# Cross attentions: contraction of 192 as 128 rows plus two rests of 64 side by side, with keys first in the first turn

## The chip, the cores and the metric

The kernel runs on one core of a Trainium2 chip. The metric is the device time of one execution in microseconds (us); lower is better. The engines of a core are called PE (matrix engine; its weight loads are PEld), DVE (vector), ACT (scalar), POOL and SP (which issues most transfers).

## The reference

A decoder of two layers works on x of shape (8, 256, 256): in layer 0 a Mamba-like block, a cross attention and a mixture of experts, in layer 1 a rotary attention, a second cross attention and a split attention, each followed by a layer norm. All is float32. What matters here is the cross attention, whose context ctx_768 has shape (8, 77, 192):

```python
q = (x @ Wq).reshape(B, Nq, 16, 64)
k = (context @ Wk).reshape(B, 77, 16, 64)
v = (context @ Wv).reshape(B, 77, 16, 64)
attn = softmax(einsum('bqhd,bkhd->bhqk', q, k) / 8)
out = einsum('bhqk,bkhd->bqhd', attn, v).reshape(B, Nq, 1024)
return out @ Wo + bo
```

Keys and values contract over the 192 columns of the context, and there are 8 x 77 = 616 context rows.

## The kernel before

The function `cross` (line 300) is called twice, once per layer. It doesn't form q or the attention's output by head. It folds Wq into the keys and Wo into the values, so that x is multiplied directly with "weighted keys" M, and the probabilities directly with "weighted values" U:

- `keys(q, part)` (line 391): the keys of two batches (2 x 77 = 154 context rows) for four pairs of heads. A pair of heads fills 128 columns of Wk. The 192 rows of the contraction are two chunks of 96 rows (`kc`), so each pair of heads takes two matmuls that add up in PSUM (L399). The result is copied by ACT with the factor 1/8 into KT (L405).
- `weighted_keys(q, g)` (line 410): for each head, 64 rows of the keys against Wq. The two heads of a pair stand on partitions 0 to 63 and 64 to 127 and run side by side on PE (`tile_position`, L417). ACT copies M (L423).
- `values(c, g)` (line 333): the same as keys, for chunk c of 128 context rows (the fifth has 104) with Wv (L342); the copy VT is done by `evac`, which alternates between ACT (L74) and DVE (L76).
- `weighted_values(c, g)` (line 351): 64 rows of VT against Wo, two heads side by side (L361). `evac` copies U, and SP writes it to DRAM (`ud`, L374), since its rows are needed by batch and not by chunk; `load_U(b)` reads a batch's rows back (L383, L387).
- `scores(u)` (L436), `turn(u)` (transposes of the probabilities, L465) and `outputs(u)` (L481) work on unit u, that is half the heads of batch u // 2, 16 units in all.

PSUM has eight banks. The pool of `cross` has two buffers of one bank (`mm`: values, outputs, the transposes of x) and three buffers of two banks (`pair`, tag `sc`: scores, keys, weighted keys and values, turn).

The order is written out by hand. The first turn (`first`, line 509) prepares chunk 0 of the values, then the keys of batches 0 and 1, and puts pieces of the stage before (`tail`) at fixed places between:

```python
first = more[-2] + [lambda k=k: (keys, weighted_keys)[k // 2](0, k % 2) for k in range(4)]
places = (4, 5, 6, 7, 7, 8, 8)
```

Here `more[-2]` is values, values, weighted values, weighted values of chunk 0. After that comes the loop over units (line 525). In iteration u it issues scores(u + 1), outputs(u - 1), then one call of keys or weighted keys for a later pair of batches, then the pieces `more[u]` of the next chunks (values in u = -1, 1, 2, 4, 5, 8, 9; weighted values in 0, 3, 4, 6, 7, 10, 11), the transposes, and `after`, which belongs to the next stage. The first attention's tail is the end of mamba: the transposes and outputs of its last steps. In mamba's last step two pairs of PSUM banks are read late, by ACT (L234) and then by DVE (L242).

The weights arrive by `cross_weights` (line 1551) on SP's queue long before they are used, Wk and Wv as 96 partitions x 2 x 1024, the context as 96 partitions x 2 x 616.

Of the kernel before, what the change touches and what calls it, by code (L numbers as in the profile page):

```python
# [10 lines left out]
F32 = mybir.dt.float32  # L11
U32 = mybir.dt.uint32
I32 = mybir.dt.int32
AF = mybir.ActivationFunctionType
# [4 lines left out]
P = 128  # L19
NB, SEQ, D = 8, 256, 256  # L20
NT = NB * SEQ
NBLK = NT // P
NCTX, DCTX = 77, 192
EPS = 1e-5
BIG = 1e30
REG = 5
# [23 lines left out]
def decoder_kernel(ctx: ExitStack, tc: tile.TileContext, a: dict, out: bass.AP):  # L50
    nc = tc.nc
# [18 lines left out]
    def evac(dst, src):  # L70

        n_evac[0] += 1
        if n_evac[0] % 2:
            nc.scalar.copy(dst, src)  # L74
        else:
            nc.vector.tensor_copy(dst, src)  # L76
# [55 lines left out]
    def weight(pool, src, k, n, p=P, parts=1):  # L132

        t = pool.tile([P, 2048], F32, tag="w", name="w")
        v = t[:p, : k * n].rearrange("p (k n) -> p k n", k=k)
        rows = src.rearrange("(k p) n -> p k n", p=p)
        for i in range(parts):
            at = slice(i * n // parts, (i + 1) * n // parts)
            nc.sync.dma_start(out=v[:, :, at], in_=rows[:, :, at])
        return v  # L140
# [159 lines left out]
    def cross(xs, W, bias, ctxT, at_unit, after, tail):  # L300
# [5 lines left out]
        wv, wo, wk, wqT = W  # L306
# [4 lines left out]
        with ExitStack() as st:  # L311
# [7 lines left out]
            def mm():  # L319
                return cps.tile([P, 512], F32, tag="mm", name="mm")  # L320

            def pair():
                return cps.tile([P, 2, 512], F32, tag="sc", name="sc", bufs=3)
# [6 lines left out]
            def span(c):  # L330
                return c * P, min((c + 1) * P, NB * NCTX)

            def values(c, g):

                lo, hi = span(c)
                if g == 0:
                    VTs[c] = c1.tile([P, 8, P], F32, tag="VT", name="VT")
                ps = mm()
                for i in range(4):
                    hp = g * 4 + i  # L340
                    for kc in range(2):
                        nc.tensor.matmul(  # L342
                            ps[:, i * P : i * P + hi - lo], wv[:, kc, hp * P : (hp + 1) * P],
                            ctxT[:, kc, lo:hi], start=kc == 0, stop=kc == 1,
                        )
                evac(
                    VTs[c][:, g * 4 : g * 4 + 4, : hi - lo],
                    ps.rearrange("p (i n) -> p i n", i=4)[:, :, : hi - lo],
                )

            def weighted_values(c, g):

# [38 lines left out]
            def keys(q, part):  # L391

                if part == 0:
                    KTs[q] = c1.tile([P, 8, 2 * NCTX], F32, tag="KT", name="KT")
                ps = pair()
                for i in range(4):
                    hp = part * 4 + i
                    for kc in range(2):
                        nc.tensor.matmul(  # L399
                            ps[:, i // 2, i % 2 * 2 * NCTX : (i % 2 + 1) * 2 * NCTX],  # L400
                            wk[:, kc, hp * P : (hp + 1) * P],
                            ctxT[:, kc, q * 2 * NCTX : (q + 1) * 2 * NCTX],
                            start=kc == 0, stop=kc == 1,
                        )
                nc.scalar.activation(  # L405
                    KTs[q][:, part * 4 : part * 4 + 4].rearrange("p (a i) n -> p a (i n)", a=2),
                    ps[:, :, : 4 * NCTX], AF.Copy, scale=0.125,
                )

            def weighted_keys(q, g):  # L410
# [90 lines left out]
            more = {}  # L501
            for c in range(NCH):
# [3 lines left out]
                        lambda c=c, k=k: (values, weighted_values)[k // 2](c, k % 2)  # L506
                    )

            first = more[-2] + [
                lambda k=k: (keys, weighted_keys)[k // 2](0, k % 2) for k in range(4)  # L510
            ]
            places = (4, 5, 6, 7, 7, 8, 8)
            for i, piece in enumerate(first):
                piece()
                for t, at in zip(tail, places):
# [1034 lines left out]

    def cross_weights(pool, i, other=None):
        return (
            weight(pool, a[f"Wv{i}"], 2, 1024, 96), weight(pool, a[f"Wo{i}"], 8, D),
            weight(pool, a[f"Wk{i}"], 2, 1024, 96), weight(other or pool, a[f"Wq{i}T"], 8, D),
        )


    with ExitStack() as st:

        wx = st.enter_context(pool_of(tc, name="wx", bufs=3, side="right"))  # L1560
        cv = const.tile([P, 4, 6], F32, name="cv")
        w_bc = const.tile([P, 4, 32], F32, name="w_bc")
        ctxT = const.tile([96, 2, NB * NCTX], F32, name="ctxT")
        cst = const.tile([P, NCONST], F32, name="cst")
        cs = {n: cst[:, lo:hi] for n, (lo, hi) in _CONST.items()}
        rw = const.tile([P, 2, 8], F32, name="rw")
        rows = {
            n: const.tile([P, a[n].shape[0]], F32, name=f"row_{n}")
            for n in ("bo0", "ebias", "b_out", "bo1", "b_proj", "g0")
        }  # L1570
        route = Route(st, rw, rows["ebias"], cs)
        with pool_of(tc, name="wq", bufs=1) as wq:
            apart = ExitStack()
            wa = apart.enter_context(pool_of(tc, name="wa", bufs=3, side="right"))
            my = apart.enter_context(pool_of(tc, name="my", bufs=3, side="right"))
            load_x(0)
            w_in = weight(wa, a["W_inT"], 2, 1024, parts=4)
            for s in range(1, 4):
                load_x(s)
            nc.sync.dma_start(out=cv, in_=a["conv"].rearrange("(c p) k -> p c k", p=P))  # L1580
            nc.sync.dma_start(out=w_bc, in_=a["W_bcT"].rearrange("(c p) n -> p c n", p=P))
            W1 = (w_in, w_bc, weight(wa, a["W_dtT"], 4, 512), weight(wa, a["W_outT"], 4, D))
            nc.sync.dma_start(out=ctxT, in_=a["ctxT"].rearrange("(k p) n -> p k n", p=96))
            for n, t in rows.items():
                nc.sync.dma_start(out=t, in_=a[n].partition_broadcast(P))
            nc.sync.dma_start(out=cst, in_=a["consts"])
            nc.sync.dma_start(out=rw, in_=a["rwT"].rearrange("(k p) n -> p k n", p=P))
            W2 = cross_weights(wx, 0, wq)
            xs, tail = mamba(xs, W1, cv, my, apart.close)
            W3 = []  # L1590

            def shared_weights(u):
                for at, n, k, w in ((4, "sw1T", 2, 1024), (8, "sw2T", 2, 1024), (14, "sw3T", 8, D)):
                    if u == at:
                        W3.append(weight(wx, a[n], k, w))

            def routed(b, n_s, nT_s, ps):
                if b % 2:
                    route.add(b // 2, n_s, nT_s, ps)
                    if b < NB - 1:  # L1600
                        route.count(b // 2, ps)

            xs, tail = cross(xs, W2, rows["bo0"], ctxT, shared_weights, routed, tail)
        layer = ctx.enter_context(ExitStack())
        attention = ExitStack()

        def begin(xs):

            wc = layer.enter_context(pool_of(tc, name="wc", bufs=1))
            w6 = wc.tile([P, 2048], F32, name="w6")  # L1610
            signs = Signs(
                w6[:, 0:1536].rearrange("p (k n) -> p k n", k=2)[:, :, 0:256], rows["g0"], cs
            )
            wb = attention.enter_context(pool_of(tc, name="w4", bufs=1))
            w4 = wb.tile([P, 2048], F32, name="w4")
            W4, W6 = [], []
            for W, w, n, lo, hi in (
                (W4, w4, "wqkT", 0, 1024), (W4, w4, "wvT", 1024, 1536),
                (W4, w4, "woT", 1536, 2048), (W6, w6, "W_qkv", 0, 1536),
                (W6, w6, "W_proj", 1536, 2048),  # L1620
            ):
                v = w[:, lo:hi].rearrange("p (k n) -> p k n", k=2)
                nc.sync.dma_start(out=v, in_=a[n].rearrange("(k p) n -> p k n", p=P))
                W.append(v)
            rotary = Rotary(attention, xs, W4, cs)
            begun.extend([rotary, signs, W6])
            return rotary.first()

        begun = []
        xs, tail = experts(xs, W3, route, tail, begin)  # L1630
# [44 lines left out]
def _arrays(i):  # L1675

    def c(v):
        return np.ascontiguousarray(v)

    i = {k: np.asarray(v) for k, v in i.items()}  # L1680
    consts, rot = _constants()
    xp = i["L0_attn_W_xproj"]
    qkv = i["L1_attn_w_qkv"]
    return {
        "x": c(i["x"]),
        "ctxT": c(i["ctx_768"].reshape(NB * NCTX, DCTX).T),
        "consts": consts,
        "rot": rot,
        "W_inT": c(i["L0_attn_W_in"].T),
# [2 lines left out]
        "W_bcT": c(xp[:32].T),  # L1692
        "W_dtT": c(xp[32:].T),
        "W_outT": c(i["L0_attn_W_out"].T),
        **{f"W{n}{l}": c(i[f"L{l}_xattn_W{n}"]) for n in "kvo" for l in (0, 1)},
        **{f"Wq{l}T": c(i[f"L{l}_xattn_Wq"].T) for l in (0, 1)},
        **{f"bo{l}": c(i[f"L{l}_xattn_bo"]) for l in (0, 1)},
        "rwT": c(i["L0_ffn_router_w"].T),
# [42 lines left out]
```

## Time and profile before

| what | value |
|---|---|
| median of 5 runs | 1464.8 us (1462.6 to 1466.49) |
| profiled execution, time | 1464.22 us |
| profiled execution, span from first to last instruction | 1461.8 us |
| PE busy | 1383.5 us (95%), 7938 matmul instructions |
| DVE, ACT, POOL busy | 834.3, 654.7 and 522.1 us |
| mean granted clock of PE | 0.989 |
| first attention, first turn | 178 to 210 us |
| first attention, loop over units | 210 to 436 us |
| second attention, first turn | 957 to 978 us |
| second attention, loop over units | 978 to about 1200 us |

In a row of the profile, L342 is line 342 of the kernel; "out<-in" are the program's own names for tiles; x16 counts instructions; a time in brackets is how long the engine stood idle before the row, and who ended that. Each float32 matmul of the program appears as two matmul instructions and two weight loads.

### The profile page before, as it was taken

How to read it: one execution, taken by the hardware profiler on the slowest of the kernel's cores; microseconds unless marked ns; L12 is line 12 of the kernel's file. 1: busy time of each engine (PE TensorE's matmuls, PEld its weight loads, DVE VectorE, ACT ScalarE, POOL GpSimd, SP SyncE). 2: the span in 40 equal slices, each digit the busy share in tenths (PEclk: the TensorE clock that was granted, in tenths of full speed). 3: DMA queues.
4: the chain of work that ended last, by engine and by line, in shares of the span. 5: the costliest groups of instructions: out<-in, count | busy, mean ns of one | idle time of the engine just before them, and what ended most of it. 6: DMA issues, size and time to landing. Idle time of an engine off the chain costs nothing.

```text
span 1461.8 us, 21959 instructions
## 1 busy us (share of the span) xinstructions
PE 1383.5 (95%) x7938; PEld 966.8 (66%) x7938; DVE 834.3 (57%) x2285; ACT 654.7 (45%) x1608; POOL 522.1 (36%) x525
## 2 busy tenths in 40 slices
PE   8999889999999999999989999999999999899996
PEld 3443478888875666656566666678888787566564
DVE  3654445554662523323658888835555563787886
ACT  3555442333432112221248878833333322877884
POOL 0333122222210123316435665432333354546541
PEclk9999999999999999999999999999999999999999
DMA  9000023324350012332130000023222210100100
GB/s 246 24 0 1 0 93 94 107 73 161 111 222 15 22 44 87 86 121 82 29 101 2 1 1 2 1 83 117 80 75 86 76 41 6 19 16 16 30 16 16
DMA packets 71679, 87.81 MB, mean 60 GB/s; under 512 B 5588, under 2 KB 66164, under 8 KB 71060
## 3 DMA queue, kind: packets, MB, share of 16 engines
q1 hardware_dynamic: 68164, 77.10, 17.6%
q0 software_dynamic: 3408, 9.31, 2.3%
q8 instruction: 64, 1.05, 0.3%
q14 instruction: 43, 0.35, 0.1%
HBM read 56.87 MB, written 29.52 MB: 59 GB/s over the span
## 4 chain that ended last, share of the span: by engine, by line
PE 74%; DVE 15%; ACT 4%; POOL 4%; issue 3%; DMA 0%; POOLq 0%; DVEq 0%; ACTq 0%
PE mm L481 9%; PE sc L436 8%; PE mm L737 7%; DVE p L990 6%; PE mm L800 5%; PE op L1027 4%; PE ps_sc L1012 4%; PE pair L229 4%; PE ps_sc L981 4%; PE tr L754 3%; PE sc L399 2%; PE tr L814 2%; PE sc L417 2%; PE sc L465 2%; PE mm L342 2%
## 5 line engine op out<-in xcount | busy, mean ns | idle before, releaser
L997 ACT ACTIVATE p<-p,nmx 128x256 f32<-128x256 f32 x512 | 253.0, 496 | 64.4 <-DVE nmx L990 64.3
L456 POOL TENSOR_TENSOR p<-p,sm 128x616 f32<-128x616 f32 x60 | 72.6, 1215 | 249.1 <-DVE sm L453 218.7
L481 PE MATMUL mm<-Ub,pT 128*128 128x256 f32 (+1 forms) x640 | 144.6, 379 | 0.5 <-ACT pT L74 0.4
L436 PE MATMUL sc<-M,xT_s 128*128 128x308 f32 x512 | 139.6, 423 | 0.8 <-ACT pT L74 0.8
L1012 PE MATMUL ps_sc<-ident,p 128*128 128x128 f32 x1024 | 133.0, 277 | 6.7 <-DVE nmx L990 4.8
L1012 PEld LDWEIGHTS ps_sc<-ident,p 128*128 128x128 f32 x1024 | 114.6, 142 | 33.3 <-issue 13.1
L481 PEld LDWEIGHTS mm<-Ub,pT 128*128 128x128 f32 (+1 forms) x640 | 120.8, 190 | 20.0 <-ACT pT L74 0.9
L737 PE MATMUL mm<-xT_s,w 128*128 128x512 f32 x256 | 116.5, 608 | 3.8 <-DVE h L743 3.0
L436 PEld LDWEIGHTS sc<-M,xT_s 128*128 128x128 f32 x512 | 94.0, 188 | 33.4 <-ACT pT L74 1.5
L449 ACT ACTIVATE p<-p 128x616 f32<-128x616 f32 x64 | 45.8, 716 | 150.0 <-DVE p L445 128.5
L990 DVE CUSTOM_DVE_ANT_0 p<-ps_sc,zero 128x256 f32<-128x256 f32 x256 | 90.7, 420 | 29.1 <-PE ps_sc L981 27.6
L990 DVE CUSTOM_DVE_ANT_0 p<-ps_sc,term 128x256 f32<-128x256 f32 x256 | 90.6, 420 | 25.8 <-PE ps_sc L981 25.7
L997 ACT ACTIVATION_READ_ACCUMULATOR p<-p,nmx 128x1 f32 x512 | 96.0, 188 | 0.0
L774 POOL DMA_INDIRECT xb<-xd,token x39 | 37.2, 954 | 147.3 <-PE tr L781 81.1
L737 PEld LDWEIGHTS mm<-xT_s,w 128*128 128x128 f32 x256 | 48.8, 195 | 59.6 <-issue 54.5
L443 DVE TENSOR_REDUCE nmx<-sc 128x8 f32<-128x616 f32 x64 | 51.1, 798 | 54.5 <-PE sc L436 54.5
L1015 DVE COPY pT<-ps_sc 128x1024 f32<-128x1024 f32 x64 | 77.6, 1213 | 3.1 <-PE ps_sc L1012 3.1
L1015 ACT COPY pT<-ps_sc 128x1024 f32<-128x1024 f32 x64 | 63.7, 996 | 26.9 <-PE ps_sc L1012 26.7
L800 PE MATMUL mm<-wE,xbT 128*128 x156 | 73.5, 593 | 0.3 <-ACT xbT L786 0.3
L741 ACT ACTIVATE g<-mm 128x512 f32<-128x512 f32 x32 | 19.1, 597 | 104.5 <-PE mm L737 93.8
L452 DVE TENSOR_REDUCE sm<-p 128x8 f32<-128x616 f32 x64 | 50.6, 790 | 22.5 <-ACT p L449 21.9
L1270 POOL TENSOR_TENSOR ssq<-ssq,nhalf 128x32 f32<-128x32 f32 x8 | 43.4, 5430 | 54.7 <-DVE ssq L1267 54.7
(287 smaller groups left out, 2676.5 us busy)
## 6 DMA issues: line engine op xcount, KB each, us to landing
Ub<-ud SPq DMA_DIRECT2D x32, 512.0 KB
ud<-U SPq DMA_DIRECT2D x16, 616.0 KB
wE<-in_wE SPq DMA_DIRECT2D x4, 1536.0 KB
yd<-y SPq DMA_DIRECT2D x39, 128.0 KB
Ub<-ud SPq DMA_DIRECT2D x32, 104.0 KB
ud<-U SPq DMA_DIRECT2D x4, 608.0 KB
x_s<-in_x SPq DMA_DIRECT2D x8, 256.0 KB
w<-in_Wo SPq DMA_DIRECT2D x2, 1024.0 KB
```

What stands on the lines that cost most here:

```text
L229: nc.tensor.matmul(ps[:, i, :], w_dt[:, kc, c * P : (c + 1) * P], xc[s][kc // 2][:, kc % 2, :], start=kc == 0, stop=kc == 3,)
L436: nc.tensor.matmul(sc[:, a, : 4 * NCTX], xT_b[:, kc, j * P : (j + 1) * P], M[:, a * 4 : a * 4 + 4, kc, at : at + NCTX], start=kc == 0, sto ...
L456: engine.tensor_tensor(pv, pv, bcast(sm, 2, [P, 8, NCTX]), ALU.mult)
L481: nc.tensor.matmul(o[:, j * D : (j + 1) * D], pT[:n, c, j * P : (j + 1) * P],  Us[b][:n, g, c], start=g == 0 and j == 0 and c == 0, stop=g ...
L737: nc.tensor.matmul(ps, w[:, kc, cols], xT_s[:, kc, :], start=kc == 0, stop=kc == 1)
L800: nc.tensor.matmul(ps, xT[:, kc, :], column(j, kc * 512, 512), start=kc == 0, stop=kc == 1)
L981: self.last_score = nc.tensor.matmul(scs[s // 2][:, s % 2, :], self.queries(b, c, s, qb), self.keys(b, c, s), start=True, stop=True, tile_ ...
L990: self.last = nc.vector.tensor_tensor_reduce(out=p[:, h, :], in0=s4[:, h, :], in1=self.term(b, qb), scale=-1.0, scalar=3.0e38, op0=ALU.add ...
L997: nc.scalar.activation(p[:, h, :], p[:, h, :], AF.Exp, bias=nmx[:, qb, n : n + 1], scale=-1.0, accum_out=sums[:, qb, n : n + 1],)
L1012: nc.tensor.transpose(tr[:, at : at + P], p[:, h, kb * P : (kb + 1) * P], ident)
L1015: (nc.scalar.copy if j else nc.vector.tensor_copy)(self.pT[b, c, j][:, :, :, qb * P : (qb + 1) * P], tr.rearrange("p (h k t) -> p h k t", ...
L1027: nc.tensor.matmul(self.op[b][s * 32 : (s + 1) * 32, c, :], va[:, kb, 8 * c + 2 * s + m, :], self.pT[b, c, s // 2][:, s % 2 * 2 + m, kb, : ...
```

## The change

The contraction of 192 is cut differently: 128 rows in one full matmul, and a rest of 64. The rests of two pairs of heads stand on partitions 0 to 63 and 64 to 127 (the rest of the context is stored twice) and run side by side as two tiles of 64 rows. A new function, `from_context`, does this for keys and values; both now use the `pair` buffers, the two pairs of heads that run side by side going to different banks. The copy of the values of chunk 0 is always on ACT. The first turn now has the order keys, keys, values, values, weighted keys, weighted keys, weighted values, weighted values, and the tail's first two pieces come behind the second values. The weights are rearranged on the host into one chunk of 128 rows with 1024 + 512 columns.

```diff
+DHEADS = 1024
...
+            def from_context(w, g, lo, hi, copy, dst):
+                n, ps = hi - lo, pair()
+                for a in range(2):
+                    at = slice(a * n, (a + 1) * n)
+                    for i in range(2):
+                        hp = g * 4 + a * 2 + i
+                        nc.tensor.matmul(
+                            ps[:, i, at], w[:, 0, hp * P : (hp + 1) * P], ctxT[:, 0, lo:hi],
+                            start=True, stop=False,
+                        )
+                    for i in range(2):
+                        rest, k = DHEADS + (g * 2 + a) * P, slice(i * 64, (i + 1) * 64)
+                        nc.tensor.matmul(
+                            ps[:, i, at], w[k, 0, rest : rest + P], ctxT[k, 1, lo:hi],
+                            start=False, stop=True, tile_position=(i * 64, 0),
+                        )
+                copy(
+                    dst[:, g * 4 : g * 4 + 4, :n].rearrange("p (a i) n -> p i a n", a=2),
+                    ps[:, :, : 2 * n].rearrange("p i (a n) -> p i a n", a=2),
+                )
...
             def values(c, g):
-                ps = mm()
-                for i in range(4):
-                    hp = g * 4 + i
-                    for kc in range(2):
-                        nc.tensor.matmul(
-                            ps[:, i * P : i * P + hi - lo], wv[:, kc, hp * P : (hp + 1) * P],
-                            ctxT[:, kc, lo:hi], start=kc == 0, stop=kc == 1,
-                        )
-                evac(
...
+                from_context(wv, g, lo, hi, nc.scalar.copy if c == 0 else evac, VTs[c])
...
             def keys(q, part):
-                ps = pair()
...
+                from_context(
+                    wk, part, q * 2 * NCTX, (q + 1) * 2 * NCTX,
+                    lambda dst, src: nc.scalar.activation(dst, src, AF.Copy, scale=0.125), KTs[q],
                 )
...
-            first = more[-2] + [
-                lambda k=k: (keys, weighted_keys)[k // 2](0, k % 2) for k in range(4)
-            ]
-            places = (4, 5, 6, 7, 7, 8, 8)
+            first = [lambda k=k: (keys, weighted_keys)[k // 2](0, k % 2) for k in range(4)]
+            first[2:2], first[6:] = more[-2][:2], more[-2][2:]
+            places = (3, 3, 6, 7, 7, 8, 8)
...
-            weight(pool, a[f"Wv{i}"], 2, 1024, 96), weight(pool, a[f"Wo{i}"], 8, D),
-            weight(pool, a[f"Wk{i}"], 2, 1024, 96), weight(other or pool, a[f"Wq{i}T"], 8, D),
+            weight(pool, a[f"Wv{i}"], 1, 1536), weight(pool, a[f"Wo{i}"], 8, D),
+            weight(pool, a[f"Wk{i}"], 1, 1536), weight(other or pool, a[f"Wq{i}T"], 8, D),
...
-        ctxT = const.tile([96, 2, NB * NCTX], F32, name="ctxT")
+        ctxT = const.tile([P, 2, NB * NCTX], F32, name="ctxT")
...
+    def two_rests(w):
+        rest = w[P:].reshape(DCTX - P, 4, 2, P).transpose(2, 0, 1, 3).reshape(P, 4 * P)
+        return c(np.concatenate([w[:P], rest], 1))
...
-        "ctxT": c(i["ctx_768"].reshape(NB * NCTX, DCTX).T),
+        "ctxT": c(np.concatenate([ctxT, ctxT[P:]])),
```

More of the change, by code (lines that the diff above doesn't have):

```diff
@@ L337, in values @@
                     VTs[c] = c1.tile([P, 8, P], F32, tag="VT", name="VT")
-                ps = mm()
-                for i in range(4):
-                    hp = g * 4 + i
-                    for kc in range(2):
-                        nc.tensor.matmul(
-                            ps[:, i * P : i * P + hi - lo], wv[:, kc, hp * P : (hp + 1) * P],
-                            ctxT[:, kc, lo:hi], start=kc == 0, stop=kc == 1,
-                        )
-                evac(
-                    VTs[c][:, g * 4 : g * 4 + 4, : hi - lo],
-                    ps.rearrange("p (i n) -> p i n", i=4)[:, :, : hi - lo],
-                )
+                from_context(wv, g, lo, hi, nc.scalar.copy if c == 0 else evac, VTs[c])
             def weighted_values(c, g):
@@ L394, in keys @@
                     KTs[q] = c1.tile([P, 8, 2 * NCTX], F32, tag="KT", name="KT")
-                ps = pair()
[L396 to L407, printed above, removed]
+                from_context(
+                    wk, part, q * 2 * NCTX, (q + 1) * 2 * NCTX,
+                    lambda dst, src: nc.scalar.activation(dst, src, AF.Copy, scale=0.125), KTs[q],
                 )
@@ L1582, in decoder_kernel @@
             W1 = (w_in, w_bc, weight(wa, a["W_dtT"], 4, 512), weight(wa, a["W_outT"], 4, D))
-            nc.sync.dma_start(out=ctxT, in_=a["ctxT"].rearrange("(k p) n -> p k n", p=96))
+            nc.sync.dma_start(out=ctxT, in_=a["ctxT"].rearrange("(k p) n -> p k n", p=P))
             for n, t in rows.items():
@@ L1678, in c @@
         return np.ascontiguousarray(v)
+    def two_rests(w):
+        rest = w[P:].reshape(DCTX - P, 4, 2, P).transpose(2, 0, 1, 3).reshape(P, 4 * P)
+        return c(np.concatenate([w[:P], rest], 1))
     i = {k: np.asarray(v) for k, v in i.items()}
+    ctxT = i["ctx_768"].reshape(NB * NCTX, DCTX).T
     consts, rot = _constants()
@@ L1694, in _arrays @@
         "W_outT": c(i["L0_attn_W_out"].T),
-        **{f"W{n}{l}": c(i[f"L{l}_xattn_W{n}"]) for n in "kvo" for l in (0, 1)},
+        **{f"W{n}{l}": two_rests(i[f"L{l}_xattn_W{n}"]) for n in "kv" for l in (0, 1)},
+        **{f"Wo{l}": c(i[f"L{l}_xattn_Wo"]) for l in (0, 1)},
         **{f"Wq{l}T": c(i[f"L{l}_xattn_Wq"].T) for l in (0, 1)},
```

## The prediction

> **What bounds the kernel now.** I read the page first, then the sums over time windows for the two cross attentions, then TensorE's (PE's) timeline there.
>
> ```profile
> PE 1383.5 (95%) x7938; PEld 966.8 (66%) x7938; DVE 834.3 (57%) x2285; ACT 654.7 (45%) x1608; POOL 522.1 (36%) x525
> PE 74%; DVE 15%; ACT 4%; POOL 4%; issue 3%; DMA 0%; POOLq 0%; DVEq 0%; ACTq 0%
> ```
>
> PE is busy 95% and carries 74% of the chain. The window sums (columns: stretch, its length, busy us of PE, PEld, DVE, ACT, POOL, granted clock, DMA share, GB/s) ask whether that holds in the stages that change. The last two rows are the unit loops of both attentions, the first three lie in the first turn of the first.
>
> ```profile
> 182.83:186.25 3.42, 1.66 (x16) 1.46 (x16) 1.23 (x1) 1.69 (x3) 2.26 (x2) 1.00 0.00 0
> 186.25:189.66 3.41, 0.34 (x4) 0.00 (x0) 1.88 (x3) 1.01 (x1) 1.82 (x2) 1.00 0.00 0
> 189.66:193.07 3.41, 3.22 (x16) 2.54 (x16) 1.26 (x2) 1.01 (x1) 2.02 (x1) 0.50 0.26 75
> 211.00:436.00 225.00, 221.90 (x1376) 186.53 (x1375) 130.58 (x252) 77.73 (x112) 50.97 (x52) 1.00 0.40 130
> 978.00:1190.00 212.00, 208.19 (x1271) 174.19 (x1270) 124.05 (x208) 67.51 (x100) 76.97 (x54) 1.00 0.30 89
> ```
>
> In the loops PE idles 3.1 us of 225 and 3.8 of 212: there every ns added to PE's stream is a ns of the kernel. After a stretch with PE busy 0.34 us of 3.41 the clock is 0.50 for the next 3.41; after 1.66 of 3.42 (49%) it stays 1.00. The first turns wait (start, length, in brackets the idle time before):
>
> ```profile
> 178.10 3.74 PE L342 MATMUL mm<-ctxT,w 96*128 96x128 f32 x32
> 184.59 2.00 PE L361 MATMUL sc<-w,VT 64*128 64x256 f32 x16 [2.75 <-ACT VT L74]
> 189.85 3.57 PE L361 MATMUL sc<-w,VT 64*128 64x256 f32 x16 [3.26 <-DVE VT L76]
> ...
> 956.67 3.74 PE L342 MATMUL mm<-ctxT,w 96*128 96x128 f32 x32
> 963.20 5.41 PE L361 MATMUL sc<-w,VT 64*128 64x256 f32 x32 [2.79 <-DVE VT L76]
> 968.54 2.36 PE L399 MATMUL sc<-ctxT,w 96*128 96x154 f32 x16
> ```
>
> The weighted values (L361) wait for copies of the values that ACT and DVE do late; part of what follows runs at half clock (189.85: 3.57 us for x16, against 2.00). Now the prices, from rows of the loop:
>
> ```profile
> 226.54 3.72 PE L361 MATMUL sc<-w,VT 64*128 64x256 f32 x32
> ...
> 240.51 2.26 PE L399 MATMUL sc<-ctxT,w 96*128 96x154 f32 x16
> 242.60 1.95 PE L342 MATMUL mm<-ctxT,w 96*128 96x128 f32 x16
> ...
> 249.63 4.48 PE L481 MATMUL mm<-Ub,pT 128*128 128x256 f32 x20
> 254.04 2.37 PE L417 MATMUL sc<-KT,w 64*128 64x154 f32 x32
> 256.34 2.05 PE L342 MATMUL mm<-ctxT,w 96*128 96x128 f32 x16
> ```
>
> ```profile
> L399 PE MATMUL sc<-ctxT,w x256: 292/294/398, 193.3 to 1128.4; 96*128 96x154 f32 x128
> L417 PE MATMUL sc<-KT,w x512: 288/291/395, 198.6 to 1159.9; 64*128 64x154 f32 x171
> ```
>
> Each f32 matmul is two instructions. A slot is the distance of two starts: L399 (2.26 - 0.294)/15 = 0.131 us, L342 (1.95 - 0.275)/15 = 0.112. L417 works on 64 rows, two heads side by side: x32 are 16 pairs, (2.37 - 0.291)/15 = 0.139 a pair, so two for hardly more than the slot of one.
>
> The rest of that row is the price of **switching** between 128 and 64 rows. Out: the last pair of 254.04 starts at 254.04 + 2.37 - 0.291 = 256.12, the next row at 256.34, 0.22 later instead of 0.131 (0.09 lost); and that row takes 2.05 for what takes 1.95 after another 128-row matmul (0.10), because the first weight load is no longer hidden: 395 ns against 291 in L417's longest. In: row 249.63 last starts at 249.63 + 4.48 - 0.380 = 253.73, L417 0.31 later instead of 0.216 (0.09), and its row is 2.37 where 15 x 0.131 + 0.291 = 2.26 (0.11). A switch costs 0.19 to 0.20 us either way; I take 0.194.
>
> The Trainium skill (TensorEngine Tiling (Array Packing), Key Properties) says that changing the tiling mode drains TensorE, without a price; the rows above show the drain and its size. The same page's Theoretical Speedup table, up to 2x for contractions of at most 64, would alone promise the gross saving below with no cost, and about -23 us in all.
>
> **The change part by part.**
>
> *Fewer slots.* A call of values or keys had 8 matmuls = 16 slots; now 4 full ones (8 slots) and 4 of 64 rows in pairs (4 slots). Values: 20 calls x 4 x 0.112 = 9.0 us; keys: 16 x 4 x 0.131 = 8.4. Together -17.3.
>
> *More switches.* from_context goes full, rest, full, rest: in, out, in, out, four switches a call, unless weighted keys or values (already on 64 rows) follow, which saves one and removes one that was there. By units of the loop, new minus old: u=-1: 8, 0: 2, 1: 8, 2: 4, 3: 0, 4: 6, 5: 8, 6 and 7: 0, 8 and 9: 8 each: 52 per attention. First turn: 20 against 6 in the first attention, 18 against 4 in the second: 14 each. 2 x (52 + 14) = 132 x 0.194 = 25.6; 14 of them lead into transposes, whose load is shorter by 0.05: 25.0. So PE's stream grows by 25.0 - 17.3 = **7.7 us**.
>
> *First turn, second attention.* Keys first, value copies all on ACT. ACT is idle from 951.5 to 960.5 and the banks are free, so keys, values, weighted keys, weighted values run through: the idle 2.79 and the half clock (PEclk 0.5 for 3.41 us, worth 1.7) go, -4.4 with 0.1 for the tail's transposes, which need POOL's last row at 965.65 when PE arrives at 965.6. Scores start at about 974.6 instead of 978.01. U's round trip through DRAM on SP's queue starts 7.2 us later: weighted keys end at 971.0, the first half of the weighted values 1.73 and its copy 1.2 later, so 974.0 instead of 966.85. Its traffic ended at 990 before and should now at 997, and outputs of unit 0 need it at 999.3 (1002.22 before). Two us to spare, so nothing.
>
> *First turn, first attention.* The pool's first tag is now the three pairs, so these get the low six banks, handed out as first, third, second (so does every three-buffer tag in the program's memory map). The second keys call falls on the banks of mamba's last step, which DVE reads late:
>
> ```profile
> 184.09 1.23 DVE L242 SCALAR_TENSOR_TENSOR y<-pair,e 128x1024 f32<-128x1024 f32 x1 [2.35 <-ACT e L240]
> ```
>
> Keys 0 end at 178.10 + 12 x 0.131 + 4 x 0.194 = 180.45; keys 1 wait until 185.37: 4.9 us idle in one piece instead of 2.75 + 3.26, -1.1. Behind this wait stands PE's whole stream. PE is then busy 30% and 25% of the stretches to 182.83 and to 186.25, so I expect half clock until 189.66: 4.3 us at half, 2.15 lost against 1.6 now, +0.5. The 0.88 us before the next values (217.05, for a bank of mm that values no longer use) goes, -0.9. Together -1.4.
>
> *At nothing.* Values now share the three pairs with scores, keys and turns. The next scores take the buffer that values filled; the VT copy ended 0.2 to 1.0 us before scores began in eleven of the twelve places behind unit 0 and 0.2 after in one; the exit switch adds 0.15 of slack. What covers the copy is the turn's transposes; without them each place would cost what the copy is late. Wk, Wv and ctxT load in other shapes; they are issued by 24 and 744 us and used from 178 and 957 on. The copies' element counts stay.
>
> *Sum:* +7.7 - 4.4 - 1.4 = **+1.9 us**. The profiled execution took 1464.22 us (span 1461.8 and 2.4 around it), 0.6 under the median of the five runs, 1464.8. On the median: **1466.7 us**, +0.13%, less than the 0.2% (2.9 us) that a measurement can tell from no change.
>
> **The rivals.**
>
> *A. Side by side no longer hides* (slower). If scores wait for VT copies because these stand behind other work on ACT or DVE, these twelve places pay. A copy lasts 0.69 us and starts 0.04 to 0.56 behind the last matmul, against 1.24 of turn and switch; from 0.55 of delay on each further 0.4 costs 12 x 0.4 = 4.8 us: 1471.5. For: three pairs carry more than before; one place was late already. Against: eleven others.
>
> *B. U comes back too late in the second attention* (slower). Decides beyond 2.0 us of further delay; a stall of 2 to 4 us there gives 1469 to 1471. For: 23 us of round trip on one queue. Against: unit 0 needs only the first half of it.
>
> *C. The first attention doesn't wait* (faster). Were the early pairs on free banks, idle 6.0, half clock 1.6 and 0.9 all go: -8.5 instead of -1.4, 1459.6. If only the first values wait, -2.8 more than I sum: 1463.9. Against: the memory map.
>
> *D. Switches are cheaper in short runs* (faster). Without the exposed load, 132 x 0.10 = 13 us less: 1453. Against: mamba's bc_p matmul (two instructions on 16 rows between 128-row ones) pays both parts in full: 0.52 us from start to start into and out of it, against 0.43, and 0.10 more each time for the load.
>
> **How the numbers follow.** Forecast and its near variants (+-2.9 us) 0.47; A 0.26; B 0.08; C fully 0.07; D 0.05; longer half-clock or other new waits in the first turns, 1468 to 1470, 0.07. Slower: 0.26 + 0.08 + 0.06 = 0.40; faster 0.13; same 0.47. The range takes in A and B to 1472 and C in part, from 1461.5; the forecast's own is 1463.8 to 1469.6.
>
> **What would show it.** PE's instruction count unchanged at 7938; x8 of 128 rows and x8 of 64 in each call; about 25 us of drains and bare loads in PE's busy time, so units with keys and values longer by 0.5 us; scores in the second attention starting 3 to 4 us earlier against mamba's end, and the kernel giving it back by the loop's end; 4.9 us idle before the second keys at 185.4. I am wrong if switches cost under 0.15 us, if PE waits for VT copies in the loop, or if keys 1 start at 180.5.

## The result, and the profile after

The changed kernel takes 1468.84 us (median of 37 runs, 1460.5 to 1470.79) against 1464.77 us for the kernel before beside it (63 runs): a ratio of 1.0025 [1.0019, 1.0032]. So it is slower, by 4.1 us where 1.9 were forecast. The time lies within the forecast's own 1463.8 to 1469.6; but the difference can be told from none, and the prediction gave that less chance (slower, 0.40) than no difference that can be told (0.47). One execution of all those in this document, of e5, took 2012 us at a mean granted clock of 0.65, and no ratio counts it. The profiled execution took 1469.53 us, 5.3 more than that of before. First the engines and the chain in the page of after:

```profile
PE 1393.6 (95%) x7938; PEld 959.5 (65%) x7938; DVE 833.2 (57%) x2283; ACT 656.3 (45%) x1610; POOL 522.6 (36%) x525
PE 73%; DVE 16%; ACT 4%; POOL 3%; issue 3%; DMA 2%; SPq 0%; POOLq 0%; DVEq 0%; ACTq 0%
```

PE has the same 7938 instructions and is busy 10.1 us longer, in a span 5.4 us longer. Where, the distances between stage borders on PE's timeline tell, for both profiled executions:

| stretch | before | after | difference | forecast |
|---|---|---|---|---|
| up to the first matmul on the context (mamba) | 178.10 | 179.53 | +1.4 | 0 |
| first attention, first turn | 32.37 | 36.93 | **+4.6** | about +0.2 |
| first attention, loop (first scores to last outputs) | 224.63 | 226.23 | +1.6 | +2.2 |
| experts and rotary attention | 521.58 | 520.75 | -0.8 | 0 |
| second attention, first turn | 21.34 | 17.66 | **-3.7** | -3.7 |
| second attention, loop | 230.79 | 232.90 | +2.1 | +3.1 |
| rest | 253.0 | 253.2 | +0.2 | 0 |

The forecast column spreads the terms of the prediction over the stretches: 14 more switches in each first turn, 52 in each loop, less the slots saved there, with the waits and half clock that belong to each. The first and the fourth row hold no changed instruction. Stretches of half clock come there at other places in each execution, always of 3.41 us or a multiple of it (called windows here): the first row has one more of them after (from 112.70 us), the fourth four instead of three, and why that is still 0.8 us shorter is not settled. The four stretches that change give +4.6 us together, near the 4.1 of the medians. One row carries the miss: the first turn of the first attention. Its timeline in after (start, length, in brackets the idle time before and who ended it; L342 full part, L348 rest, L421 weighted keys, L89 transposes):

```profile
180.61 0.79 PE L342 MATMUL sc<-ctxT,w 128*128 128x154 f32 x4
181.33 0.53 PE L348 MATMUL sc<-ctxT,w 64*128 64x154 f32 x4
186.81 1.40 PE L342 MATMUL sc<-ctxT,w 128*128 128x154 f32 x4 [4.94 <-DVE y L243]
...
191.09 1.22 PE L342 MATMUL sc<-ctxT,w 128*128 128x128 f32 x4
...
198.61 1.97 PE L89 MATMUL mm<-ident,x_s 128*128 128x128 f32 x8
```

The wait is the forecast one: 4.94 us before the second keys, for DVE's late read of mamba's last buffer. But behind it every row has nearly twice its length (1.40 for the 0.79 of the same row ahead of the wait), and that lasts for all of the keys and values. The window sums of after say why (stretch, length, busy us of PE, PEld, DVE, ACT, POOL, granted clock, DMA share, GB/s):

```profile
181.00:184.38 3.38, 0.87 (x8) 0.47 (x6) 1.42 (x2) 3.35 (x3) 1.79 (x2) 1.00 0.00 0
184.38:187.79 3.41, 0.98 (x4) 0.98 (x4) 1.23 (x1) 1.11 (x2) 2.26 (x2) 0.50 0.00 0
187.79:191.21 3.42, 3.42 (x15) 2.18 (x14) 1.42 (x2) 0.68 (x2) 1.83 (x2) 0.50 0.02 5
191.21:194.62 3.41, 3.41 (x16) 2.73 (x16) 0.00 (x0) 0.68 (x1) 1.91 (x1) 0.50 0.01 2
194.62:198.03 3.41, 3.41 (x18) 2.51 (x16) 0.00 (x0) 0.58 (x1) 0.00 (x0) 0.50 0.00 0
198.03:201.45 3.42, 3.42 (x19) 2.86 (x21) 0.00 (x0) 1.75 (x3) 0.00 (x0) 0.50 0.00 0
201.45:204.86 3.41, 3.41 (x52) 3.36 (x52) 0.00 (x0) 3.06 (x6) 0.00 (x0) 1.00 0.00 0
```

The clock is 0.50 for five windows, 17.1 us, though PE counts as busy in all of the last four. Before, the full clock came back after one such window (189.66 to 193.07 in the prediction's rows). The second attention and the loop in after:

```profile
246.07 0.69 PE L342 MATMUL sc<-ctxT,w 128*128 128x154 f32 x4
...
250.46 1.31 PE L469 MATMUL sc<-ident,p 128*128 128x128 f32 x10
...
963.45 0.69 PE L342 MATMUL sc<-ctxT,w 128*128 128x154 f32 x4
...
965.71 0.79 PE L342 MATMUL sc<-ctxT,w 128*128 128x154 f32 x4
...
968.08 0.71 PE L342 MATMUL sc<-ctxT,w 128*128 128x128 f32 x4
...
972.33 0.69 PE L89 MATMUL mm<-ident,x_s 128*128 128x128 f32 x4
...
981.11 4.42 PE L440 MATMUL sc<-M,xT_s 128*128 128x308 f32 x16
```

A keys and a values call in one unit take 250.46 - 246.07 = 4.39 us; before, the same two took 244.39 - 240.51 = 3.88. That is +0.51, the 0.5 forecast for such a unit. In the second attention everything from the first keys (963.45) to the scores (981.11) runs through in 17.66 us without a wait.

### The profile page after: what moved, and what is told of

Read it like the earlier page. It is cut to its first block, busy times and chain, and to the rows that moved or that the text cites. A ratio compares the mean times of both kernels' runs of the same rounds, so it can differ in the third digit from the quotient of the medians.

```text
span 1467.2 us, 21969 instructions
## 1 busy us (share of the span) xinstructions
PE 1393.6 (95%) x7938; PEld 959.5 (65%) x7938; DVE 833.2 (57%) x2283; ACT 656.3 (45%) x1610; POOL 522.6 (36%) x525
## 3 DMA queue, kind: packets, MB, share of 16 engines
q1 hardware_dynamic: 67972, 77.26, 16.8%
## 4 chain that ended last, share of the span: by engine, by line
PE 73%; DVE 16%; ACT 4%; POOL 3%; issue 3%; DMA 2%; SPq 0%; POOLq 0%; DVEq 0%; ACTq 0%
PE mm L485 9%; PE sc L440 8%; PE mm L740 7%; DVE p L993 6%; PE mm L803 5%; PE op L1030 4%; PE ps_sc L1015 4%; PE pair L230 4%; PE ps_sc L984 4%; PE sc L342 3%; PE tr L757 3%; DVE acc L193 2%; PE tr L817 2%; PE sc L421 2%; PE sc L469 2%
## 5 line engine op out<-in xcount | busy, mean ns | idle before, releaser
L1000 ACT ACTIVATE p<-p,nmx 128x256 f32<-128x256 f32 x512 | 253.0, 496 | 64.9 <-DVE nmx L993 64.7
L993 DVE CUSTOM_DVE_ANT_0 p<-ps_sc,term 128x256 f32<-128x256 f32 x256 | 90.7, 420 | 26.5 <-PE ps_sc L984 26.4
```

Of the source, the lines that this page charges most:

```text
L993: self.last = nc.vector.tensor_tensor_reduce(out=p[:, h, :], in0=s4[:, h, :], in1=self.term(b, qb), scale=-1.0, scalar=3.0e38, op0=ALU.add ...
L1000: nc.scalar.activation(p[:, h, :], p[:, h, :], AF.Exp, bias=nmx[:, qb, n : n + 1], scale=-1.0, accum_out=sums[:, qb, n : n + 1],)
```

## The experiments

Two rounds of four kernels, each round with the kernel before beside it on its chip (1465.21 us in the first, 1464.6 in the second). A mode switch is counted wherever two matmuls that follow each other on PE use tiles of another size (128, 64 or 32 rows or columns): before 263, after 395, the forecast 132 more.

**e1: the order alone.** The kernel before, with its two chunks of 96 rows, and only the new order and the copies on ACT:

```diff
-            first = more[-2] + [
-                lambda k=k: (keys, weighted_keys)[k // 2](0, k % 2) for k in range(4)
-            ]
-            places = (4, 5, 6, 7, 7, 8, 8)
+            first = [lambda k=k: (keys, weighted_keys)[k // 2](0, k % 2) for k in range(4)]
+            first[2:2], first[6:] = more[-2][:2], more[-2][2:]
+            places = (3, 3, 6, 7, 7, 8, 8)
...
-                evac(
+                (nc.scalar.copy if c == 0 else evac)(
```

> The new order of the first turn alone (keys first, weighted values last, value copies of chunk 0 on ACT), with the old two chunks of 96 rows and values in the mm buffers. Theory T (the time is PE's stream: 0.194 us a switch of the row mode, against the slots saved): no switches added, loops as before within 0.5 us, second attention's first turn 16.8 instead of 21.3 us; in the first attention the second keys wait until DVE's late read as they do in the changed kernel (5.2 us idle). Theory H (the half clock after that wait lasted 17 us in the changed kernel because switches thin out PE's stream): a dense stream ends it within 3.4 to 6.8 us, first turn of the first attention 32 to 33 us, total 1460.2 (-4.6). If the length of the wait alone made it long: half clock about 17 us here too, first turn about 36, total 1464.5. Rival W (the cost lies in values on the shared pair buffers and copies over two banks): 1460.2 as well.

Measured: 1460.16 us (12 runs), 0.9967 [0.9955, 0.9979]. The order gains 5.0 us. In the profile 3.7 of that is the second attention's first turn (17.68 us, as in after, where 16.8 were expected: PE waits 0.9 us there for POOL's rows of the tail's transposes); the first attention's hardly changes (32.11 against 32.37 before). There PE waits 5.02 us before the second keys, as long as after does, and yet the clock is back after 6.8 us:

```profile
185.76 4.35 PE L399 MATMUL sc<-ctxT,w 96*128 96x154 f32 x16 [5.02 <-DVE y L242]
189.94 3.73 PE L342 MATMUL mm<-ctxT,w 96*128 96x128 f32 x32
```

The keys at 185.76 are at half clock (2.26 for the same row at 178.48), the values at 189.94 already at full (3.73, as in the prediction's row at 178.10).

**e2: the cut alone.** After, with the old order and places and `evac` for all value copies (the minus lines of e1's diff put back).

> The new cut alone (128 rows plus rests of 64) with the old order of the first turn and copies alternating as before. T: 132 - 2 = 130 switches more than before, +7.7 us of PE stream, and the second attention keeps its wait for DVE's copy (about 2.8 us): 1472.5. H: the second values now wait for DVE's late read, and a thinned stream follows: half clock over 10 us, 1475 to 1477. If the order costs and the cut gains: under 1464.8. W: 1470 to 1473, and PE waiting in the loops.

Measured: 1464.09 us (12 runs), 1.0005 [0.999, 1.002]: no difference that can be told, where a clear loss was expected. Its loops are longer by 1.7 and 2.0 us against before, as in after; its first turns by +1.6 and -1.6. That is +3.6 in the stretches that change, and the untouched experts and rotary stretch gives it back in this execution: it is 4.3 us shorter than in the profile of before, which had three windows of half clock there against one in e2. Over all runs the mean clock is 0.989 against 0.988, worth about 1.5 us of 1465; why the windows fall better in e2 than in before is not settled. Besides, the expectation put a longer half clock into the first turn, and it lasted 10.2 us, shorter than after's 17.1: dense weighted values (from 188.79 on) follow behind two values calls there. Two windows of e2:

```profile
186.00:189.40 3.40, 3.40 (x18) 2.64 (x19) 1.77 (x3) 0.00 (x0) 1.80 (x2) 0.50 0.02 5
189.40:192.80 3.40, 3.40 (x20) 2.70 (x18) 0.68 (x2) 1.01 (x1) 2.08 (x1) 0.50 0.01 2
```

Alone, the order gains 5.0 us and the cut costs nothing that can be told; together they lose 4.1. The two parts interact. Two theories for that: the long wait alone puts the clock down for long (then e1 should show it; it doesn't), or the stream behind the wait, broken by switches, keeps it down.

**e3: grouped.** After, but each call does its four full matmuls first and then the four rests, two switches instead of four:

```diff
-            def from_context(w, g, lo, hi, copy, dst):
+            def from_context(w, g, lo, hi, copy, dst, turned=False):
...
+                def whole(start):
+                    for a in range(2):
+                        at = slice(a * n, (a + 1) * n)
+                        for i in range(2):
...
-                            start=True, stop=False,
+                                start=start and a == 0, stop=not start and a == 1,
...
+                def rests(start):
...
-                            start=False, stop=True, tile_position=(i * 64, 0),
+                                start=start and a == 0, stop=not start and a == 1,
+                                tile_position=(i * 64, 0),
...
+                for part, start in zip((rests, whole) if turned else (whole, rests), (True, False)):
+                    part(start)
```

> As the changed kernel, but in each call all four full matmuls first and then all four rests: two switches a call, 72 fewer than the changed kernel, same matmuls, same buffers, same copies. T: 1468.8 - 72 x 0.194 = 1454.9. H adds that the half clock in the first attention's first turn gets shorter (under 10 us instead of 17), worth up to 4 us more: 1451. W (buffers and copies cost, not switches): 1468.8, no change.

Measured: 1454.1 us (6 runs), 0.9929 [0.9913, 0.9946], 14.7 us under after for 72 switches fewer. In the loop of the first attention 28 fewer switches take 226.23 to 220.79 us: 5.44 / 28 = 0.194 us each, the price that the prediction read from rows of before. The first scores and the last outputs of that loop, in after:

```profile
216.47 4.31 PE L440 MATMUL sc<-M,xT_s 128*128 128x308 f32 x16
438.11 4.59 PE L485 MATMUL mm<-Ub,pT 128*128 128x256 f32 x20 [0.40 <-ACT pT L75]
```

and in e3:

```profile
209.79 4.31 PE L450 MATMUL sc<-M,xT_s 128*128 128x308 f32 x16
425.99 4.59 PE L495 MATMUL mm<-Ub,pT 128*128 128x256 f32 x20 [0.40 <-ACT pT L75]
```

In the second loop only 3.2 of the expected 5.4 us show in the length; PE's idle time there is 5.3 us of 210 against after's 3.1 of 212, so 2.2 us turned into waits. And the half clock ends after 6.8 us, behind a wait of 5.34 (windows of e3):

```profile
183.31:186.72 3.41, 0.89 (x3) 0.89 (x4) 1.23 (x1) 1.20 (x2) 2.26 (x2) 0.50 0.00 0
186.72:190.14 3.42, 3.42 (x17) 2.80 (x17) 1.41 (x2) 1.19 (x2) 1.83 (x2) 0.50 0.02 5
190.14:193.55 3.41, 3.41 (x34) 2.92 (x34) 0.00 (x0) 0.95 (x3) 2.02 (x1) 1.00 0.01 2
```

W, which put the cost on buffers and copies, is out, since e3 has after's. That the total lies so near T's 1454.9 is partly luck. In the profile the first attention's first turn shrinks by 5.7 us (36.93 to 31.23), some 4 more than its eight switches are worth, as H said. But the second attention's, also with eight switches fewer, does not shrink at all (17.68 against 17.66), since PE now waits 1.3 us there for POOL's rows of the tail's transposes. What H adds and what these waits take back nearly cancel.

**e4: grouped and turned.** e3, and where two calls follow each other the second begins with its rests (`turned`), so that no switch lies between them (36 fewer again):

```diff
-                from_context(wv, g, lo, hi, nc.scalar.copy if c == 0 else evac, VTs[c])
+                from_context(
+                    wv, g, lo, hi, nc.scalar.copy if c == 0 else evac, VTs[c], c > 1 or g == 1
+                )
...
-                    lambda dst, src: nc.scalar.activation(dst, src, AF.Copy, scale=0.125), KTs[q],
+                    lambda dst, src: nc.scalar.activation(dst, src, AF.Copy, scale=0.125), KTs[q],
+                    q == 0 and part == 1,
```

> As e3_grouped, but every second call begins with its rests where the call before ended with them: 108 switches fewer than the changed kernel, only 24 more than before. T: 1468.8 - 108 x 0.194 = 1447.9, so some 17 us (1.2%) under the kernel before; H: half clock shorter, down to 1444. W: 1468.8.

Measured: 1453.31 us (6 runs), 0.992 [0.9902, 0.9937], 5.4 us above what was expected. The first loop gave its share, 220.79 to 218.62 us for 14 switches (0.155 each; several of them lead into transposes, whose load is shorter). The second attention did not: its first turn takes 19.13 us instead of 17.68, because PE arrives too early at the tail's transposes. The waits of PE between 950 and 985 us in e4 (what waited, for whom: us in total, times, longest):

```profile
PE mm L89 <- POOL x_s L117: 1.9, 2, 1.1
PE sc L387 <- DVE U L77: 0.8, 1, 0.8
```

A window of half clock follows the first of them, at 957.7; another, at 988.4, stands behind this 0.8 and a further wait of 1.83 us for the copy of U. A saving ahead of a fixed arrival became waits and slow windows. Over all six executions the mean clock is 0.984 to 0.988, against 0.989 or 0.990 in e3; 0.004 of 1453 us are 5.8, about what is missing. Two of the windows more lie in the experts in this execution, so not all of it is explained.

**e5: without most of the wait.** After, with mamba's first two transposes ahead of the keys in the first attention, so that the first buffers of both tags are taken in another order and the late-read bank falls to a later call:

```diff
-            places = (3, 3, 6, 7, 7, 8, 8)
+            places = (-1, -1, 6, 7, 7, 8, 8) if len(tail) > 2 else (3, 3)
+            for t, at in zip(tail, places):
+                if at == -1:
+                    t(mm())
```

> As the changed kernel, but in the first attention two of mamba's transposes are issued ahead of the keys, so that the mm buffers get the low banks and the pairs the others: both keys calls fall on free banks and only the first values wait for DVE's late read at 185.4. Switches the same. Theory TH (0.194 us a switch, and a half clock that the wait starts and the thinned stream prolongs): idle 1.7 us instead of 4.9, no 17 us of half clock, first turn of the first attention 27.6 instead of 36.9 us, total 1459.5. If the wait matters but not the half clock behind it: 1468.8 - 3.2 = 1465.6. W (buffers and copies): 1465.6 or more.

Measured: 1462.28 us (11 runs), 0.9988 [0.9976, 1.0], 6.6 us under after but 2.8 above what was expected. The wait is down to 1.70 us, the first turn from 36.93 to 29.06; 0.9 us of that is only the two transposes, which now stand ahead of the first keys. The expectation counted on no half clock; the values behind this short wait still ran at half for 6.8 us (timeline and windows of e5):

```profile
185.25 0.71 PE L342 MATMUL sc<-ctxT,w 128*128 128x128 f32 x4 [1.70 <-DVE y L243]
```

```profile
182.81:186.22 3.41, 1.71 (x15) 1.17 (x13) 1.22 (x1) 2.08 (x4) 2.26 (x2) 0.99 0.00 0
186.22:189.63 3.41, 3.37 (x18) 2.45 (x14) 1.41 (x2) 1.74 (x3) 1.82 (x2) 0.50 0.00 0
```

**e6: grouped, turned and ahead.** e4 and e5 together, and the second attention's transposes put two calls later, behind the weighted keys, to give POOL's rows time (`else (5,)` for `else (3, 3)`).

> e4_turned with the transposes ahead as in e5_ahead, and in the second attention the tail's transposes behind the second weighted keys, since PE waited 1.9 us there for POOL's rows and went to half clock. TH: first turn of the first attention 26.3 us instead of 30.6, of the second 16 instead of 19.1: 1445.4, the fastest. If only the idle time counts: 1453.3 - 3.6 - 1.9 = 1447.8. W: no difference to e4_turned beyond the idle time.

Measured: 1446.19 us (4 runs), 0.988 [0.9864, 0.9895]: faster than both kernels, 18.4 us under before and 0.8 from what was expected. The wait for POOL's rows is gone, the second attention's first turn is down to 15.59 us. The wait for mamba's bank in the first attention, in e6:

```profile
185.20 1.99 PE L344 MATMUL sc<-ctxT,w 128*128 128x128 f32 x8 [2.70 <-DVE y L243]
```

**e7: the order and the transposes ahead, old cut.** e1 with the diff of e5.

> e1_order (old cut into 96 + 96) with the transposes ahead. TH: first turn of the first attention 27 instead of 32.1 us: 1455.1; so e6_turned_ahead is 10 us faster than this one by fewer slots (-17.3) against 24 to 26 switches (+5) and what the clock adds. If the cut gave nothing: equal.

Measured: 1455.02 us (5 runs), 0.9934 [0.992, 0.9947], as expected. Here no half clock follows at all: the first turn takes 25.61 us, or 26.5 with the two transposes ahead of it, the shortest of all, with a wait of 1.27:

```profile
184.62 3.84 PE L342 MATMUL mm<-ctxT,w 96*128 96x128 f32 x32 [1.27 <-ACT xT_s L93]
```

So of e6's 18.4 us the order and the transposes' place bring 9.6, and the cut, once grouped and turned, 8.8 more. Up to 0.9 of these 8.8 is not the cut's: e7 keeps the second attention's transposes at their place in after and waits 0.9 us there for POOL's rows. By the terms, 17.3 of slots less 30 more switches than e7 (289 against 259), 30 x 0.194 = 5.8, would be 11.5. Part of the difference lies in the first attention's first turn, 26.96 us in e6 against 25.61: PE waits 2.70 us there and 3.4 us of half clock follow. Another part lies in the second loop, where PE waits 6.5 us in e6 and 5.0 in e7, most of it for copies of U.

**e8: grouped in the first attention's first turn alone.** After, with e3's grouping only in the four calls of this turn, one ahead of the wait and three behind it (`grouped = q == 0 and len(tail) > 2`, for values `c == 0 and len(tail) > 2`): 8 switches fewer than after, the wait kept.

> The changed kernel with the four calls of the first attention's first turn grouped (all full matmuls, then all rests): 8 switches fewer, at half clock some 2 us, the wait of 4.9 us before the second keys stays, all else the same. TH: half clock behind the wait 6.8 us instead of 17.1 as in e3_grouped, first turn 36.9 - 5.5 = 31.4 us, total 1463.2, mean clock up from 0.984 to 0.988. If the long wait alone sets the half clock: 17 us stay, and 1467.2 remains.

Measured: 1461.44 us (11 runs), 0.9975 [0.9966, 0.9984], 7.4 us under after and 1.8 under what TH gave. This separates the two theories. The wait is even longer than after's (5.34), and the half clock lasts 3.4 us instead of 17.1 (timeline and windows of e8):

```profile
185.34 2.42 PE L343 MATMUL sc<-ctxT,w 128*128 128x154 f32 x8 [5.34 <-DVE y L243]
187.69 1.23 PE L352 MATMUL sc<-ctxT,w 64*128 64x154 f32 x8
188.85 1.16 PE L343 MATMUL sc<-ctxT,w 128*128 128x128 f32 x8
...
192.32 1.09 PE L89 MATMUL mm<-ident,x_s 128*128 128x128 f32 x8
193.34 4.67 PE L439 MATMUL sc<-KT,w 64*128 64x154 f32 x64
```

```profile
181.80:185.21 3.41, 0.00 (x0) 0.00 (x0) 1.15 (x1) 2.22 (x2) 2.35 (x1) 1.00 0.00 0
185.21:188.62 3.41, 3.28 (x14) 2.97 (x16) 0.95 (x3) 0.68 (x1) 2.35 (x1) 0.50 0.02 5
188.62:192.03 3.41, 3.41 (x34) 2.89 (x34) 0.54 (x1) 1.27 (x2) 2.35 (x1) 1.00 0.01 2
```

The eight switches are worth at most 8 x 0.194 = 1.6 us at full clock; the first turn shrank by 6.1 (36.93 to 30.79). The other 4.6 are half clock that the order of eight matmuls within a call decides. The wait starts the half clock; the broken stream keeps it.

That it lasts 3.4 us here and 6.8 in e3, behind the same wait and the same calls, is where the windows fall: in e8 one begins at 185.21, just before the wait ends, in e3 the wait ends at 185.83, 2.5 us into one. In after it ends 2.4 us into one, as in e3, so of the four windows by which after and e8 differ one is luck and three are not. A single trace could mislead here, but the mean clock of the other executions agrees: 0.989 to 0.991 in all 11 of e8, 0.981 to 0.986 in 34 of the 39 of after whose clock is on record, and the two kernels differ in nothing else. The other five of after have 0.988 to 0.991 and take 1460.5 to 1466.8 us.

## Why the prediction was right in most steps and wrong in one

**Switches and slots: right.** PE's instructions are 7938 as said, the program has 132 more switches as counted, and 0.194 us a switch is what 28 of them gave in e3. The loops grew by 1.6 and 2.1 us where the terms make 2.2 and 3.1. What is missing is idle time that the longer stream of PE covered: PE idled 3.1 and 3.8 us in the windows of the loops before and idles 1.6 and 3.1 now (0.9 of the first is the gap that the prediction takes out). The windows of after:

```profile
217.00:442.00 225.00, 223.41 (x1373) 182.60 (x1372) 129.73 (x250) 77.62 (x112) 50.98 (x52) 1.00 0.41 135
982.00:1194.00 212.00, 208.91 (x1263) 168.98 (x1262) 123.00 (x206) 66.98 (x99) 76.01 (x53) 1.00 0.31 96
```

So the prediction erred a little high here: it let the switches add in full and forgot that a stream that gets longer waits less for the others.

**Second attention's first turn: right.** -3.7 forecast (the -4.4, and 0.7 for 14 switches less the slots), -3.68 measured.

**First attention's first turn: the wait right, its price wrong.** Rival C is out: the memory map was read rightly, and keys 1 stood 4.94 us for 4.9 forecast. The step that failed is "I expect half clock until 189.66: 4.3 us at half, 2.15 lost". It took from one row of before that one window of work releases the clock. Measured, the half clock lasted to 201.45. The loss, by rows of after at half and at full clock (those from 965.71 to 972.33 in its second attention): keys 4.28 against 2.37 us, each values call 3.76 against 2.12; the eight transposes take 1.90 against 1.02 in e8, and the weighted keys 0.4 more than in the second attention: 6.5 us in sum. That is 4.4 more than the 2.15, and the stretch missed by 4.4.

What keeps the clock down can be put in a number, an estimate from slots: at half clock a slot is about twice 0.131 or 0.112 us (e1's row of keys takes 4.35 us at half and 2.26 at full). The keys call at 186.81 has 12 slots, 12 x 0.262 = 3.14 us of its 4.28, 73%; a values call 12 x 0.224 = 2.69 of 3.76, 72%. The rest is drains and bare loads, which the rows still count as busy. Three windows of after filled with such calls did not release the clock; its fourth (198.03 to 201.45, mostly transposes and weighted keys, about 89%), e8's first (3.14 of 3.51, with the idle start about 86%), e1's (96% and more) and before's did. Windows that mix thin and dense rows lie close together by this estimate, 79% in e2 (not released) and 81% in e5 (released). So grouping decides, which e8 shows; that the share of streaming time is the measure, and where its threshold lies, is only argued from these estimates.

The Trainium skill (TensorE: Matmul & The Clock Gate, What's actually happening) says that the full clock comes after at least one busy window of about 3.4 us. The windows of 3.41 us are in these rows, and e1, e3 and e8 come near it, with one or two. After does not: of its four windows with PE busy all the time, three passed before one released the clock. So the busy time of the profile can't be what decides here.

**Rival A: refuted, by after's own trace.** The price of late VT copies was not paid. The waits of PE in the window of the second loop (what waited, for whom: us in total, times, longest), with none for VT; in the first loop there is none either (with the faster streams of e3 and e6 one of 0.4 and 0.7 us does appear in the second loop):

```profile
PE sc L469 <- DVE U L77: 2.3, 3, 1.0
PE sc L375 <- DVE U L77: 0.8, 1, 0.8
```

**Rival B: did not occur.** No wait for `Ub` stands at the second attention's first outputs. **Rival D: refuted.** The bare load is there in short runs too. The rests in after (instructions, durations in ns as least, median and most):

```profile
L348 PE MATMUL sc<-ctxT,w x288: 272/353/621, 180.2 to 1136.0; 64*128 64x154 f32 x64, 64*128 64x128 f32 x64, 64*128 64x104 f32 x16
```

The median mixes three sizes and both clocks, so take one size at full clock: of the 64 instructions on 154 columns in the second attention 32 last about 290 ns and 32 about 395, the usual and the longest duration of L417 before. The drawn-out matmul behind an unhidden load, which L417 had only in its longest ones, is every second instruction in runs of two pairs. And e3's 0.194 us a switch is the full price, not the 0.09 without the load.

**The sum.** +1.9 forecast, +4.6 in the four stretches: 4.4 more in the first turn, 1.6 less in the loops. That the time still lies in the forecast's range owes something to luck, since the two errors have opposite signs. The 0.07 given to "longer half-clock or other new waits in the first turns, 1468 to 1470" was the case that came; it deserved more, since all the switches of that turn stood behind the one wait, and the chance of the likeliest case, with its half clock taken from a denser stream, less.

## What to carry to other kernels

Count mode switches as work: in this kernel each costs 0.16 to 0.19 us, and 132 of them took back more than the 17 us of slots that the change saved (both loops grew, by 1.6 and 2.1 us). Order the matmuls within a call so that those of one mode stand together, and let the next call begin in the mode in which the last one ended. Behind any wait long enough to lower the clock put the densest stream there is, and price a wait as its idle time plus the half clock until a dense window has passed. Which call meets a late-read PSUM bank is decided by the order of first use of the buffers, so a small piece that only shifts that order can be worth a good deal: two transposes put ahead brought 5.1 us from e1 to e7 and 6.6 from after to e5. And look at what arrives at a fixed time: the second attention's first turn takes 17.66 us in after without a wait, and still 17.66 to 17.68 in e1, e3 and e7, whose shorter streams wait for POOL's rows, until e6 moves the piece that needs them.

## What was not expected of the hardware

With drains and bare loads in its stream, PE stayed at a granted clock of 0.50 for 17.1 us, four windows of it without a recorded idle time; the same work behind a longer wait took 3.4 us (e8) or 6.8 (e3) to come back when its eight matmuls a call were sorted by mode. And waits shorter than a window are no protection: 1.70 us in e5 and 2.70 in e6 (6.8 and 3.4 us of half clock) were followed by it, 1.27 in e7 was not. Why the windows of half clock in mamba and the experts, which no edit touches, come at other places in each execution stays open.
